# A four-layer graph network on one Trainium2 core: the transposed input comes from 32-feature pieces and VectorE instead of TensorE

## The chip, the cores and the metric

One Trainium2 chip, one of its cores. The metric is the device time of the one launch in microseconds (us). The kernel before takes 2986.86 us (median of three runs, 2981.26 to 2988.62); the profiled execution spans 2982.9 us.

## What is computed

The input `x` has 64 graphs of 256 nodes with 256 features, float32, and `adj` 64 adjacency matrices of 256 by 256, int32. Four layers follow each other, each wrapped as `x = layernorm(x + layer(x))`. Cut to what matters:

```python
# layer 0: masked attention with 8 heads of 32, then a feed-forward part
qkv = x @ Wqkv.T + bqkv
attn = softmax(where(allowed, q k^T / sqrt(32), -inf))
y = layernorm(x + (attn @ v) @ Wo.T + bo)
y = layernorm(y + relu(y @ W1.T + b1) @ W2.T + b2)
# layers 1 and 2: graph attention, e_ij = leaky_relu(f_i + g_j), softmax over neighbours
# layer 3: two relational convolutions with elu
```

The change touches only the first line of layer 0. A matrix product on TensorE sums over the partitions of its two operands, so `x @ Wqkv.T` needs `x` with features on the partitions, while a plain load of `x` puts nodes there. Somewhere `x` has to be turned.

## The kernel before

Each graph is worked out on its own: 256 nodes are two tiles of 128 partitions (`NB = 2`) and 256 features are two blocks of 128 (`KB = 2`). The function `graph(g)` writes down the operations of one graph with, for each, its engine, an assumed cost, the tiles it reads and the tiles it writes. `main_path` does so for all 64 graphs, and `Plan.schedule` then lists the operations of all graphs together in one order. It is a greedy list scheduler that runs while the program is built: each engine takes the ready operation with the earliest due time (graph number times `PERIOD`, less what has to follow), provided that a buffer is free in the ring of each tile it starts. On TensorE it prefers operations of the same mode ("full", "row", "col"). What comes out is a fixed order for each engine's queue; on the chip the engines run these queues in order, with semaphores between them. So operations of several graphs stand interleaved on every engine, and the sizes of the rings (`RINGS`, buffers per tile name) decide how far the graphs may overlap.

The parts of a graph that the change and the prediction touch, with the lines of the profile:

- `load("x", ...)` and `load("adj", ...)` (L582): one 256 KB transfer each, issued from the SyncE queue, rows of 1 KB.
- `masks(adj)` (L643 to L665): `bits` on VectorE (L648), four bfloat16 transposes on TensorE (L653), masks `gm` and `am` on VectorE (L656, L657, L662).
- `transposed(xt)` (L599 to L610): four 128x128 float32 transposes on TensorE into one PSUM bank (L606), and one ScalarE copy of 128x512 to a tile of ring `T` (L609). A graph calls it six times: on `x`, on the attention's output, on the inputs of both graph attentions and of both convolutions. 64 graphs make 384 calls.
- `add_row_later(xt, bo, ...)` (L591): the bias row is added to `x` by an accumulating transfer from the GpSimd queue. `x` is read again only at the end of the attention (L750).
- `projections(xT)` (L667 to L691): twelve products with `Wqkv` on the transposed input, the first TensorE work of a graph that depends on it (L615, names `T,wqkv` and `wqkv,T`).
- `attention` (L693 to L742), `feed_forward` (L753 to L775), where a second copy of `x`, `xr`, gets the row `ln2b` by another accumulating transfer and is added at L597; `gat` (L777 to L814) with tiles `e`, `h` and, in layer 2, `n`; `conv` (L852 to L895).

After the main path a check of ranges (L924 to L937) decides whether a slow general path runs. With these inputs it doesn't; the constants `ones_b` and `eye` are used there alone.

Of the kernel before, what the change touches and what calls it, by code (L numbers as in the profile page):

```python
# [8 lines left out]
F32 = mybir.dt.float32  # L9
F32R = mybir.dt.float32r  # L10
BF16 = mybir.dt.bfloat16
I32 = mybir.dt.int32
# [5 lines left out]
P = 128  # L18
# [3 lines left out]
NO_EDGE = -346.0  # L22


RINGS = {"x": 3, "adj": 4, "bits": 2, "am": 2, "gm": 6, "T": 5, "qk": 2, "v": 2, "p": 12, "both": 4, "inv": 1, "ctxT": 2, "X": 9,
         "xr": 2, "hid": 1, "h": 3, "e": 4, "n": 2, "rel": 3, "hi": 2, "lo": 2, "o": 4}
SMALL = {"mv": 8, "st": 4, "rstd": 8, "r": 6, "rdeg": 4}


# [21 lines left out]
class Plan:  # L51
# [29 lines left out]
    def op(self, engine, cost, issue, graph, reads=(), writes=(), takes=(), mode=None, port=None, lag=None):  # L81


        o = Op(engine, cost, mode, graph, issue, port, lag)
        for accesses, writing in ((reads, False), (writes, True)):
            for a in accesses:
                t, part = a if isinstance(a, tuple) else (a, None)
                write = writing
                if t.ring == "bank":
                    write, part = True, None  # L90
                keys = [k for k in t.parts if part is None or k is None or k == part]
                for k in keys:
                    writer, readers = t.parts[k]
                    o.before.update(readers if write else ())
                    if writer is not None:
                        o.before.add(writer)
                if write:
                    if part is None:
                        t.parts = {}
                    t.parts[part] = (o, [])  # L100
                else:
                    for k in keys or [part]:
                        t.parts.setdefault(k, (None, []))[1].append(o)
                if t not in o.tiles and t.ring is not None:
                    o.tiles.append(t)
        o.tiles += [t for t in takes if t not in o.tiles]
        for t in o.tiles:
            t.left += 1
        o.before.discard(o)
        for b in o.before:  # L110
            b.after.append(o)
        self.ops.append(o)
# [96 lines left out]
def tile_gnn_stack(ctx: ExitStack, tc: tile.TileContext, t: dict, out: bass.AP):  # L209
# [16 lines left out]
    nc = tc.nc  # L226
    x_in, adj_in = t["x"], t["adj"]
    B, N, D = x_in.shape
    assert N == 2 * P and D == 2 * P and B % 2 == 0
    G = B // 2  # L230
    KB = D // P
# [40 lines left out]
    gen = Stage()  # L272
# [6 lines left out]
    def load(st, view, dtype, tag, bufs=1):  # L279
        xt = st.tok(dtype, tag, bufs)  # L280
        nc.sync.dma_start(xt, view)
        return xt
# [15 lines left out]
    def cols(name, n):  # L298

        w = const.tile([P, n], F32, tag=f"col_{name}", name=f"col_{name}")  # L300
        nc.gpsimd.dma_start(w, t[name][0 : n * P].rearrange("(c p) -> p c", p=P))
        return w

    def filled(shape, dtype, tag, value):
        w = const.tile(shape, dtype, tag=tag, name=tag)
        nc.vector.memset(w, value)
        return w
# [13 lines left out]

    ident_b = const.tile([P, P], BF16, tag="ident_b", name="ident_b")
    nc.vector.tensor_copy(ident_b, ident)
    ones_b = filled([P, P], BF16, "ones_b", 1.0)
    ones = filled([P, HD], F32, "ones", 1.0)
    neghalf = filled([P, NT], F32, "neghalf", -0.5)
    eye = filled([P, N // P, N], BF16, "eye", 0.0)
    for h in range(N // P):
        nc.vector.tensor_copy(eye[:, h, h * P : (h + 1) * P], ident_b)
    gcol, bcol = cols("ln1_g", KB), cols("ln1_b", KB)  # L330
    bq = const.tile([P, KB], F32, tag="bq", name="bq")
    nc.vector.tensor_scalar(bq, bqkv[:, 0:KB], scale, None, op0=ALU.mult)
# [11 lines left out]
    for i in (1, 2):  # L344
        a = const.tile([P, 2, KB], F32, tag=f"a{i}", name=f"a{i}")
# [137 lines left out]
    def main_path(plan):  # L483
        x_graph = x_in.rearrange("g (h p) d -> g p h d", p=P)
        adj_graph = adj_in.rearrange("g (h p) m -> g p h m", p=P)
        out_graph = out.rearrange("g (h p) d -> g p h d", p=P)

        def ring(name, bufs):
            plan.ring(name, bufs, lambda shape, dtype, i: pools["work"].tile(shape, dtype, tag=f"{name}{i}", name=name))

        for name, bufs in RINGS.items():
            ring(name, bufs)
# [65 lines left out]
        def graph(g):  # L558
            def op(engine, cost, issue, reads, writes, takes=(), mode=None, port=None, lag=None):
                plan.op(engine, cost, issue, g, reads, writes, takes, mode, port, lag)  # L560

            def pe(mode, cost, issue, reads, writes, takes=()):
                op("PE", cost, issue, reads, writes, takes, mode)
# [4 lines left out]
            def act(cost, issue, reads, writes):  # L568
                op("ACT", cost, issue, reads, writes)
# [4 lines left out]
            def new(ring, shape, dtype=F32):  # L574
                return plan.tile(ring, shape, dtype)

            def tok(ring, dtype=F32):
                return new(ring, [P, NB, D], dtype)

            def load(ring, view, dtype):  # L580
                xt = tok(ring, dtype)
                op("SP", 0.85, lambda: nc.sync.dma_start(xt(), view), [], [xt])  # L582
                return xt
# [9 lines left out]
            def add_row_later(xt, row, reads=()):  # L593
                add_later(xt, lambda: row[:, None, :].to_broadcast([P, NB, D]), reads)
# [4 lines left out]
            def transposed(xt):  # L599

                xT, pt = new("T", [P, KB, N]), new("bank", [P, KB, N])

                def issue():
                    for kb in range(KB):
                        for i in range(NB):
                            nc.tensor.transpose(pt()[:, kb, i * P : (i + 1) * P], xt()[:, i, kb * P : (kb + 1) * P], ident)  # L606

                pe("full", 0.44, issue, [xt], [pt], [xT])
                act(0.47, lambda: nc.scalar.copy(xT(), pt()), [pt], [xT])  # L609
                return xT  # L610

            def product(dst, lhs, rhs, n):
# [203 lines left out]
            def layer1(xt, gm):  # L816
                def finish(i, z, po, r):
                    dve(0.40, lambda: nc.vector.scalar_tensor_tensor(z()[:, i, :], po()[:, 0:D], r(), xt()[:, i, :],
                                                                     op0=ALU.mult, op1=ALU.add), [po, r, xt], [(z, i)])


                z = gat(xt, 0, gm, 2 * g, gbias, finish)
                layer_norm(z)
                return z
# [17 lines left out]
            def relation(adj):  # L842


                rel, other = tok("rel", F32R), tok("e")
                dve(0.33, lambda: nc.vector.tensor_scalar(rel(), adj(), 1.0, None, op0=ALU.is_equal), [adj], [rel], "uses")
                dve(0.60, lambda: nc.vector.scalar_tensor_tensor(
                    other(), adj(), 1.0, rel().bitcast(F32), op0=ALU.not_equal, op1=ALU.mult,
                    accum_out=seen_rel[:, g : g + 1]), [adj, rel], [other], "uses")
                return rel  # L850
# [43 lines left out]
                    [n, o], [o], "uses")  # L894
                return o  # L895

            xt, adj = load("x", x_graph[g], F32), load("adj", adj_graph[g], I32)
            am, gm = masks(adj)
            xT = transposed(xt)
            add_row_later(xt, bo, [c_bo])  # L900
            ctxT = attention(xT, am)
            x1 = product_plus(lambda c: ctxT()[:, c, :], [ctxT, c_wo], lambda c: wo[:, c, :], KB, xt)
            layer_norm(x1)
            xt = feed_forward(x1, load("xr", x_graph[g], F32))
            xt = layer1(xt, gm)
            xt = layer2(xt, gm)
            rel = relation(load("adj", adj_graph[g], I32))
            rdeg = new("rdeg", [P, NB])
            h = conv(conv(xt, 0, rel, rdeg), 1, rel, rdeg)
# [5 lines left out]
        for g in range(B):  # L915
            graph(g)
# [185 lines left out]

    wrong = nc.values_load(bad_i, min_val=0, max_val=4 * P)
    with tc.tile_pool(name="general", bufs=1) as pools["work"], tc.If(wrong > 0):
        w_rel0 = []
        for i in (1, 2):
            w = gen.sb([P, KB, D], F32, f"w_rel0{i}")
            nc.scalar.dma_start(w, t[f"w_rel{i}"][0].rearrange("(c p) n -> p c n", p=P))
            w_rel0.append(w)
        with tc.For_i(0, G) as g:  # L1110
            xt = load(gen, x_view[bass.ds(g, 1)], F32, "x")
            xr = load(gen, x_view[bass.ds(g, 1)], F32, "xr")
            adj = load(gen, adj_view[bass.ds(g, 1)], I32, "adj")
            ctxT = general_attention(transposed(gen, xt), general_mask(adj))
            add_row(xt, bo)
            xt = feed_forward(gen, attention_end(gen, xt, ctxT), xr)
            xt = general_layer1(xt, adj)
            xt = general_layer2(xt, adj)
            xt = general_layer3(xt, adj, w_rel0)
            nc.sync.dma_start(out_view[bass.ds(g, 1)], xt)  # L1120
# [48 lines left out]
```

## Time and profile before

| | before |
|---|---|
| time, median of 3 | 2986.86 us |
| span of the profiled execution | 2982.9 us, 46.6 us for a graph |
| TensorE busy | 2930.1 us, 98% |
| VectorE busy | 2381.6 us, 80% |
| ScalarE busy | 1615.9 us, 54% |
| GpSimd busy | 870.6 us, 29% |
| mean granted TensorE clock | 0.996 |
| moved by DMA | 127.14 MB, 126767 packets |

Every instruction of the profile carries the line of kernel.py that issued it; L615 is the line of nearly all products, so names of operands tell them apart (`bank<-T,wqkv` is a product of the transposed input and the projection weights). A float32 product shows as two records for each instruction of the program, a transpose as one. "Idle before" is the time for which an engine stood still just ahead of a group, with the instruction whose end released it. Records of consecutive matmuls overlap, so the time that a group holds TensorE is read from one group's start to the next group's start in the timeline, not from the sum of durations.

### The profile page before, as it was taken

What the parts mean: (1) busy time and instruction counts of PE and PEld (TensorE: products, weight loads), DVE (VectorE), ACT (ScalarE), POOL (GpSimd) and SP (SyncE); (2) the same over time, 40 slices, a digit from 0 to 9 for tenths busy, and PEclk for the clock granted to TensorE, in tenths of its full rate; (3) what the DMA queues carried; (4) which work ended last, traced back from release to release, by engine and by line L of the source; (5) the groups of instructions that cost most, each with busy time, mean ns of one, the idle gap of its engine ahead of it and who ended that gap; (6) DMA issues with size and microseconds to landing.
All of it is one profiled execution on the core that took longest, in us unless ns stands there. A gap on an engine that the chain in (4) does not pass through costs nothing.

```text
span 2982.9 us, 49733 instructions
## 1 busy us (share of the span) xinstructions
PE 2930.1 (98%) x17462; PEld 2257.1 (76%) x17462; DVE 2381.6 (80%) x6112; ACT 1615.9 (54%) x3905; POOL 870.6 (29%) x2005
## 2 busy tenths in 40 slices
PE   7999999999999999999999999999999999999997
PEld 6777777777777877777777777777777777777884
DVE  5778788788878787878888788787887878879678
ACT  3555555555545555555555555555555554656454
POOL 2232332222232222223322223232232332322232
PEclk9999999999999999999999999999999999999999
DMA  6111121111111211112112111121121211212100
GB/s 166 42 40 44 40 47 39 41 43 36 43 44 28 50 33 47 36 36 51 42 37 47 34 42 43 47 43 30 39 49 41 44 32 40 47 43 44 26 8 23
DMA packets 126767, 127.14 MB, mean 43 GB/s; under 512 B 7697, under 2 KB 125713, under 8 KB 126513
## 3 DMA queue, kind: packets, MB, share of 16 engines
q1 hardware_dynamic: 91072, 89.15, 9.9%
q0 software_dynamic: 35440, 34.76, 8.0%
q8 instruction: 141, 2.31, 0.3%
q14 instruction: 114, 0.93, 0.1%
HBM read 73.54 MB, written 16.78 MB: 30 GB/s over the span
## 4 chain that ended last, share of the span: by engine, by line
PE 82%; DVE 10%; ACT 3%; POOL 3%; issue 1%; DMA 0%; POOLq 0%; DVEq 0%; ACTq 0%
PE bank L615 65%; PE bank L606 5%; PE bank L877 4%; PE bank L709 3%; PE bank L734 3%; PE bank L729 2%; DVE inv L738 1%; ACT X L636 1%; POOL rstd L630 1%; DVE st L624 1%; DVE p L717 1%; PE bank L797 1%; DVE mv L626 1%; DVE o L887 1%; POOL rstd L631 1%
## 5 line engine op out<-in xcount | busy, mean ns | idle before, releaser
L629 POOL TENSOR_SCALAR rstd<-mv 128x2 f32<-128x2 f32 x384 | 108.8, 283 | 1534.1 <-DVE mv L626 1303.8
L636 ACT ACTIVATE X<-X,rstd 128x256 f32<-128x256 f32 x640 | 349.7, 596 | 277.1 <-POOL rstd L632 197.9
L615 PE MATMUL bank<-T,w 128*128 128x256 f32 x2048 | 477.6, 380 | 1.1 <-ACT p L715 1.1
L615 PE MATMUL bank<-cw,T 128*128 128x512 f32 x1024 | 466.6, 598 | 8.8 <-ACT T L609 6.2
L615 PE MATMUL bank<-w,hid 128*128 128x256 f32 x2048 | 461.9, 380 | 1.0 <-ACT p L715 1.0
L615 PEld LDWEIGHTS bank<-w,hid 128*128 128x128 f32 x2048 | 384.1, 190 | 57.6 <-issue 4.6
L615 PEld LDWEIGHTS bank<-T,w 128*128 128x128 f32 x2048 | 377.0, 190 | 52.6 <-ACT T L609 3.3
L717 DVE TENSOR_TENSOR p<-p,am 128x512 f32<-128x512 f32 x512 | 334.2, 681 | 45.1 <-ACT p L715 44.3
L615 PEld LDWEIGHTS bank<-cw,T 128*128 128x128 f32 x1024 | 190.5, 190 | 209.4 <-issue 179.4
L715 ACT ACTIVATE p<-bank 128x512 f32<-128x512 f32 x512 | 300.5, 598 | 48.2 <-PE bank L709 47.8
L630 POOL TENSOR_TENSOR rstd<-rstd,neghalf 128x2 f32<-128x2 f32 x384 | 309.1, 805 | 31.9
L609 ACT COPY T<-bank 128x512 f32<-128x512 f32 x384 | 220.5, 589 | 176.9 <-PE bank L606 174.0
L767 ACT ACTIVATE hid<-bank,col_b 128x256 f32<-128x256 f32 x512 | 210.5, 477 | 118.9 <-PE bank L615 117.9
L615 PE MATMUL bank<-T,wqkv 128*128 128x256 f32 x1024 | 249.0, 386 | 3.5 <-ACT T L609 3.5
L615 PE MATMUL bank<-h,e 128*128 128x259 f32 x1024 | 247.8, 383 | 1.6 <-POOL rstd L632 1.5
L615 PE MATMUL bank<-gw,T 128*128 128x258 f32 x1024 | 247.5, 383 | 1.5 <-ACT T L609 1.3
L624 DVE BATCH_NORM_STATS2 st<-X 128x6 f32<-128x256 f32 x640 | 238.1, 413 | 2.9
L738 DVE RECIPROCAL inv<-bank 128x256 f32<-128x256 f32 x128 | 219.4, 1731 | 13.9 <-PE bank L734 13.9
L615 PEld LDWEIGHTS bank<-h,e 128*128 128x128 f32 x1024 | 190.8, 190 | 52.0 <-issue 23.7
L615 PEld LDWEIGHTS bank<-gw,T 128*128 128x128 f32 x1024 | 190.1, 190 | 39.4 <-issue 7.4
L864 ACT CAST hi<-bank 128x256 fp32r<-128x256 f32 x256 | 95.1, 372 | 228.4 <-PE bank L615 227.0
L615 PEld LDWEIGHTS bank<-T,wqkv 128*128 128x128 f32 x1024 | 190.8, 193 | 34.5 <-ACT T L609 4.8
(124 smaller groups left out, 5028.9 us busy)
## 6 DMA issues: line engine op xcount, KB each, us to landing
adj<-in_adj_dram SPq DMA_DIRECT2D x128, 256.0 KB, 2.8
x<-in_x_dram SPq DMA_DIRECT2D x64, 256.0 KB, 2.7
xr<-in_x_dram SPq DMA_DIRECT2D x64, 256.0 KB, 2.7
xr<-row_ln_b POOLq DMA_DIRECT2D x64, 256.0 KB, 3.9
x<-row_bo POOLq DMA_DIRECT2D x64, 256.0 KB, 4.3
out_dram<-o SPq DMA_DIRECT2D x64, 256.0 KB, 2.1
w<-in_W1T_dram SPq DMA_DIRECT2D x1, 1024.0 KB, 11.1
w<-in_W2T_dram SPq DMA_DIRECT2D x1, 1024.0 KB, 19.4
```

The costliest lines, as they stand in the source:

```text
L606: nc.tensor.transpose(pt()[:, kb, i * P : (i + 1) * P], xt()[:, i, kb * P : (kb + 1) * P], ident)
L609: act(0.47, lambda: nc.scalar.copy(xT(), pt()), [pt], [xT])
L615: nc.tensor.matmul(dst, lhsT=lhs(c), rhs=rhs(c), start=(c == 0), stop=(c == n - 1))
L624: nc.vector.bn_stats(stat()[:, i, :], y()[:, i, :])
L629: nc.gpsimd.tensor_scalar(rstd()[:, 0, :], mv()[:, :, 1], 1.0, EPS, op0=ALU.mult, op1=ALU.add)
L630: nc.gpsimd.tensor_tensor(rstd()[:, 0, :], rstd()[:, 0, :], neghalf[:, 0:NB], op=ALU.pow)
L636: nc.scalar.activation(y()[:, i, :], y()[:, i, :], AF.Identity, bias=rstd()[:, 1, i : i + 1], scale=rstd()[:, 0, i : i + 1])
L715: act(0.58, lambda pr=pr, k=k, sr=s[r]: nc.scalar.activation(pr(), sr(), AF.Exp, accum_out=seen_sum[:, k : k + 1]), [s[r]], [pr])
L717: dve(0.60, lambda pr=pr, kt=kt: nc.vector.tensor_tensor(pr(), pr(), am()[:, kt, None, :].to_broadcast([P, KB, N]), op=ALU.mult), [pr, am] ...
L738: dve(1.62, lambda hg=hg, pc=pc: nc.vector.reciprocal(inv()[:, hg, :], pc()[:, 1, :]), [pc], [(inv, hg)])
L767: act(0.36, lambda f=f, k=k, ph=ph: nc.scalar.activation(hid()[:, f + k, :], ph()[:, k, :], AF.Relu, bias=b1[:, f + k : f + k + 1]), [ph, ...
L877: nc.tensor.matmul(pa()[:, 0:n], lhsT=rel()[:, i, j * P : (j + 1) * P], rhs=part()[:, i, 0:n], start=(c == 0), stop=(c == len(terms) - 1))
```

## The change

The input is turned on the way in. For each of four partition blocks `a` and two feature blocks `kb`, one transfer of 32 KB reads 32 features of all 256 nodes: `blocks[32a + r, kb, m, c]` gets node `32m + r`, feature `128 kb + 32a + c`. Each piece of 32 features is a packet of 128 bytes. One VectorE instruction then transposes every 32x32 block of the 128x512 tile, which puts features on partitions and nodes along the row: the wanted `xT`. TensorE's four transposes and ScalarE's copy for `x` go; the other five calls of `transposed` in a graph stay. `x` itself is still loaded with nodes on partitions for the residual, but later in the graph's list, after the masks.

The new tiles `blocks` (one buffer) and `xT` (two) take room, and rings shrink: `x` 3 to 2, `T` 5 to 4, `X` 9 to 8, `xr` 2 to 1, `e` 4 to 3, `n` 2 to 1. The constants `ones_b` and `eye` move to the general path.

```diff
-RINGS = {"x": 3, ..., "T": 5, ..., "X": 9,
-         "xr": 2, ..., "e": 4, "n": 2, ...}
+RINGS = {"x": 2, ..., "T": 4, ..., "X": 8,
+         "xr": 1, ..., "e": 3, "n": 1, ..., "blocks": 1, "xT": 2}
...
-    ones_b = filled([P, P], BF16, "ones_b", 1.0)
...
-    eye = filled([P, N // P, N], BF16, "eye", 0.0)
...
+            def input_transposed():
+                blocks, xT = new("blocks", [P, KB, N // 32, 32]), new("xT", [P, KB, N])
+                for a in range(4):
+                    for kb in range(KB):
+                        f = kb * P + 32 * a
+                        op("SP", 0.51, lambda a=a, kb=kb, f=f: nc.sync.dma_start(
+                            blocks()[32 * a : 32 * a + 32, kb], x_in[g, :, f : f + 32].rearrange("(m r) c -> r m c", r=32)),
+                           [], [(blocks, 4 * kb + a)])
+                dve(0.62, lambda: nc.vector.transpose(xT().rearrange("p k n -> p (k n)"), blocks().rearrange("p k m c -> p (k m c)")),
+                    [blocks], [xT], "uses")
+                return xT
...
-            xt, adj = load("x", x_graph[g], F32), load("adj", adj_graph[g], I32)
+            xT = input_transposed()
+            adj = load("adj", adj_graph[g], I32)
             am, gm = masks(adj)
-            xT = transposed(xt)
+            xt = load("x", x_graph[g], F32)
             add_row_later(xt, bo, [c_bo])
```

More of the change, by code (lines that the diff above doesn't have):

```diff
@@ L22 @@
 NO_EDGE = -346.0
-RINGS = {"x": 3, "adj": 4, "bits": 2, "am": 2, "gm": 6, "T": 5, "qk": 2, "v": 2, "p": 12, "both": 4, "inv": 1, "ctxT": 2, "X": 9,
-         "xr": 2, "hid": 1, "h": 3, "e": 4, "n": 2, "rel": 3, "hi": 2, "lo": 2, "o": 4}
+RINGS = {"x": 2, "adj": 4, "bits": 2, "am": 2, "gm": 6, "T": 4, "qk": 2, "v": 2, "p": 12, "both": 4, "inv": 1, "ctxT": 2, "X": 8,
+         "xr": 1, "hid": 1, "h": 3, "e": 3, "n": 1, "rel": 3, "hi": 2, "lo": 2, "o": 4, "blocks": 1, "xT": 2}
 SMALL = {"mv": 8, "st": 4, "rstd": 8, "r": 6, "rdeg": 4}
@@ L323, in tile_gnn_stack @@
     nc.vector.tensor_copy(ident_b, ident)
-    ones_b = filled([P, P], BF16, "ones_b", 1.0)
     ones = filled([P, HD], F32, "ones", 1.0)
     neghalf = filled([P, NT], F32, "neghalf", -0.5)
-    eye = filled([P, N // P, N], BF16, "eye", 0.0)
-    for h in range(N // P):
-        nc.vector.tensor_copy(eye[:, h, h * P : (h + 1) * P], ident_b)
     gcol, bcol = cols("ln1_g", KB), cols("ln1_b", KB)
@@ L1104, in tile_gnn_stack @@
     with tc.tile_pool(name="general", bufs=1) as pools["work"], tc.If(wrong > 0):
+        ones_b = gen.sb([P, P], BF16, "ones_b")
+        nc.vector.memset(ones_b, 1.0)
+        eye = gen.sb([P, N // P, N], BF16, "eye")
+        nc.vector.memset(eye, 0.0)
+        for h in range(N // P):
+            nc.vector.tensor_copy(eye[:, h, h * P : (h + 1) * P], ident_b)
         w_rel0 = []
```

## The prediction, made before the changed kernel had run

> **What bounds the kernel now.** I read the busy table first, then the chain of work that ended last, then what TensorE waited for, and at last the timeline around the instructions that go. The page gives the first two:
>
> ```profile
> PE 2930.1 (98%) x17462; PEld 2257.1 (76%) x17462; DVE 2381.6 (80%) x6112; ACT 1615.9 (54%) x3905; POOL 870.6 (29%) x2005
> ...
> PE 82%; DVE 10%; ACT 3%; POOL 3%; issue 1%; DMA 0%; POOLq 0%; DVEq 0%; ACTq 0%
> PE bank L615 65%; PE bank L606 5%; PE bank L877 4%; PE bank L709 3%; PE bank L734 3%; PE bank L729 2%; DVE inv L738 1%; ACT X L636 1%; POOL rstd L630 1%; DVE st L624 1%; DVE p L717 1%; PE bank L797 1%; DVE mv L626 1%; DVE o L887 1%; POOL rstd L631 1%
> ```
>
> TensorE is busy 98% of the span: it is idle 2982.9 - 2930.1 = 52.8 us. The chain runs 82% on TensorE, and no transfer is on it. "Busy" may hide pipelining, so the waits decide. The table of waits of TensorE alone (waiter, releaser: us in total, times, longest):
>
> ```profile
> PE bank L615 <- ACT T L609: 11.0, 14, 1.9
> PE bank L615 <- DVE ctxT L739: 7.6, 1, 7.6
> PE bank L606 <- DMA x<-in_x_dram: 6.2, 1, 6.2
> PE bank L615 <- ACT p L715: 4.9, 9, 1.1
> ```
>
> Two of the four are single waits in the first 50 us (7.6 and 6.2). Between 50 and 2900 us all waits of TensorE together are 19.6 us, 0.7% of that stretch. So in steady state the kernel lasts as long as TensorE's queue is, and a microsecond taken from that queue is worth a microsecond, as long as nothing else becomes late. The groups of TensorE, shapes kept apart, show what the input's transposition is there:
>
> ```profile
> L615 PE MATMUL bank<-T,wqkv 128*128 128x256 f32 x1024 | 249.0, 386 | 3.5 <-ACT T L609 3.5
> L606 PE MATMUL bank<-ident,x 128*128 128x128 f32 x256 | 39.5, 278 | 6.6 <-DMA x<-in_x_dram 6.2 <-PE bank L709 0.4
> ```
>
> 256 transposes, four for each graph, and projections that waited 3.5 us for the copy of a transposed input. The 278 ns are a duration with overlap; what a group of four occupies is read in the timeline (start, length, what):
>
> ```profile
> 482.81 0.60 PE L606 MATMUL bank<-ident,x 128*128 128x128 f32 x4
> 483.24 1.03 PE L615 MATMUL bank<-wo,ctxT 128*128 128x256 f32 x4
> ```
>
> From 482.81 to 483.24 is 0.43 us. Other groups of the same kind read 0.44, a few 0.49 to 0.54 where the work before or after is of another tile mode.
>
> [...] No VectorE transpose is in the trace before. [...]
>
> **Part by part.**
>
> *Removed from TensorE*: 64 groups at 0.44 us = 28.2 us, on the path (98% busy). With the waits of projections for the copy, 3.5 us, it is 31.7 us. The products keep their number: the built program has the same counts of every other TensorE instruction. Its order is new, since the scheduler ran again. In it the tile mode changes 363 times against 376, and the share of the remaining transposes that are followed closely by their own product is about the same (nearly half in both). I read that as an order as dense as before and count nothing for it.
>
> *Removed from ScalarE*: 64 copies of 0.589 us = 37.7 us. ScalarE is busy 54%; worth nothing directly.
>
> *Added to VectorE*: 64 transposes of 128x512. Nearest rows: a one-input operation of that size takes 0.42 us (L891), a two-input one 0.68 us (L717). [...] I take 0.68: 43.5 us, and 2425 us busy, 82%. The bounds are 27 us (0.42) and twice my value, 87 us (84%). All stay below TensorE's 2900, so this lies beside TensorE's work. VectorE's queue is in order: if a transpose waits for its pieces, the masks, softmax products and layer norms of other graphs stand behind it. But `blocks` is refilled as soon as the previous transpose has read it and a graph has 46.6 us, and `xT` has two buffers, so a transpose can run a graph ahead of its projections. Moving `ones_b` and `eye` saves VectorE under 1 us at the start, beside the wait for the first loads.
>
> *Added to the queues*: eight transfers per graph on SyncE at about 0.37 us of issue, as `x` takes there = 3 us of 46.6; that queue mostly waits for buffers. Each has 256 packets, 16 on each DMA engine. Price of a packet: at least q1's 9.9% x 16 x 2982.9 us / 91072 = 52 ns, at most q0's 8.0% x 16 x 2982.9 / 35440 = 108 ns. Eight transfers then hold an engine 128 x 52 to 108 ns = 6.6 to 13.8 us per graph. DMA goes from 18% busy in steady state to 32 to 48%. It is hidden behind the other graphs' TensorE work. In the built order a transfer also waits for the landing of the eighth before it; `x` landed in 3.9 us (median), and eight issues take 3 us, so such a wait is at most a microsecond or two, with nothing urgent behind it.
>
> *Moved*: `x` is loaded later and gets its bias row without waiting for the transposes (the accumulating transfers waited 28.0 us for L606). It is read only after attention: hidden.
>
> *The start*: TensorE began at 6.2 us and its projections at 8.7. Now eight pieces are issued where one load was: about 0.5 us each there, and the eighth waits for `wqkv` to land (4.6 us after 0.74). Last issue near 6, landing near 9, transpose 0.7: projections near 10. The weights' loads stand behind them, some 4 us later. I put +3 us, bounds +1 and +8.
>
> *Rings*: `X` 8, `e` 3, `xr` 1, `n` 1, and a fuller VectorE queue let the graphs overlap less. This is what the profile cannot price. Floor 0; I take a third more of the 19.6 us of steady waits, +6 us.
>
> Sum: 2986.86 - 28.2 - 3.5 + 3 + 6 = 2964.2, so **2964 us**, 0.8% faster.
>
> **Rivals.**
> *The freed time comes back as waits.* Tighter rings make TensorE wait for what a ready tile of another graph used to cover. TensorE's waits for the copy L609 averaged 11.0 / 14 = 0.79 us. A wait like that in two graphs of three is 64 x 0.67 x 0.79 = 34 us: 2986.9 - 31.7 + 3 + 34 = 2992, no change. For it: six rings shrink, and layer 2's single `n` puts its two halves behind each other. Against it: the ordering was made with these rings, and TensorE's order shows no more mode changes. Chance 0.11.
> *Slower: a wait in every graph.* Late pieces stop VectorE's queue, or the single `xr` stops SyncE's and with it the masks' loads. 1.5 waits of 0.79 us per graph are 76 us: 2986.9 - 31.7 + 3 + 76 = 3034; one per graph, 51 us, gives 3009. For it: SyncE is in order and waits often; VectorE at 82% has little slack to catch up. Against it: SyncE's waits before were for buffers, and TensorE waited for a transfer once only, at the start. Chance 0.09.
> *Nothing is added in steady state*: 2986.9 - 31.7 + 1 = 2956. It is the good end of my forecast.
>
> **The numbers.** My forecast 0.80, the first rival 0.11, the second 0.09. 0.3% is 9 us: faster is below 2978, slower above 2996. So faster 0.80, same 0.11, slower 0.09. The range: 2954 (the good end and 2 us) to 2984 (28 us given back instead of 9, between forecast and first rival), which leaves out most of the rivals and a few hundredths below.
>
> **What would show it.** The group L606 with `x` gone, and TensorE's busy time near 2930 - 28 = 2902 with its share still 98%; 64 VectorE transposes near 0.68 us; ScalarE down 38 us; DMA share up by 14 to 30 points with no transfer in TensorE's waits after the first 50 us; waits of TensorE in the middle near 25 us. I am wrong if those waits reach 50 us, with releasers such as `e`, `n`, X or `xT`, or if VectorE's idle time is mostly before the new transpose, ended by the pieces' transfers.

## The result, and the profile after

The changed kernel takes 2941.67 us (median of 4 runs, 2939.83 to 2943.03) against 2984.06 us (4 runs, 2978.51 to 2988.62) for the kernel before on the same chip: a ratio of 0.9858, 95% interval 0.9838 to 0.9878. That is 42 us, 1.4% faster. The forecast was 23 us and the measured time lies below its range. The direction was right and the size was off by nearly a factor of two, so the question of this study is where the other 20 us came from.

The busy table and the chain of the changed kernel, beside those of before:

```profile
span 2939.3 us, 50120 instructions
...
PE 2894.3 (98%) x17206; PEld 2224.7 (76%) x17206; DVE 2415.6 (82%) x6172; ACT 1585.1 (54%) x3841; POOL 861.4 (29%) x2005
...
PE 84%; DVE 8%; POOL 3%; ACT 2%; issue 1%; DMA 1%; SPq 1%; POOLq 0%; DVEq 0%; ACTq 0%
```

TensorE is still the bound at 98%. Its busy time fell by 35.8 us, more than the 28 us of the transposes, and its idle time fell too, from 52.8 to 45.0 us. In the table of TensorE's waits (waiter, releaser: us in total, times, longest) the single wait for the input of the first graph has grown and the wait for `ctxT` at the start has all but gone. Between 90 and 2800 us all waits together fell from 19.3 to 13.6 us:

```profile
PE bank L625 <- DVE xT L618: 11.5, 1, 11.5
PE bank L625 <- ACT T L605: 6.8, 11, 0.9
PE bank L602 <- ACT X L646: 3.6, 8, 1.3
PE bank L602 <- ACT p L725: 3.3, 4, 1.4
...
PE bank L625 <- DVE ctxT L749: 0.6, 1, 0.6
```

(L625 is the line of products, L602 that of transposes, L605 the copy to `T`, as L615, L606 and L609 were before.) The groups on TensorE and VectorE that the change touched, with busy time, mean ns and idle time before them:

```profile
L625 PE MATMUL bank<-xT,wqkv 128*128 128x256 f32 x1024 | 252.8, 386 | 12.8 <-DVE xT L618 11.5 <-ACT T L605 1.4
L618 DVE STREAM_TRANSPOSE xT<-blocks 128x512 f32<-128x512 f32 x64 | 45.0, 703 | 8.7 <-DMA blocks<-in_x_dram 8.1 <-issue 0.4 <-DMA adj<-in_adj_dram 0.2
```

The projections wait for the new transpose once, at the start, and never after. VectorE's transpose takes 703 ns and waits for its pieces in three graphs only (8.1 us in all). The pieces are small on the DMA engines too:

```profile
q1 hardware_dynamic: 230336, 105.96, 13.8%
...
blocks<-in_x_dram SPq DMA_DIRECT2D x512, 32.0 KB, 2.0
```

From 91072 packets at 9.9% of 2982.9 us to 230336 at 13.8% of 2939.3 us: 16 x (405.6 - 295.3) us over 139264 packets is 12.7 ns for each packet more. A piece landed in 2.0 us.

To see when the time was won, I compared the moments at which both traces had finished the same amount of TensorE work (each record counted at the usual distance to its follower, the transposes of `x` at zero). After 90 us the changed kernel is about 6 us ahead; from there to 2890 us the lead grows, unevenly, to 43 us, on average 0.6 us for each graph. A graph's four transposes occupy 0.44 us, 28 us in all. So by this account some 6 us were won at the start, 28 by the transposes, and 9 by something else, of which the shorter waits of the middle are 5.7.

The granted TensorE clock differs too. Over the first 90 us it was 0.92 before and 0.96 in the changed kernel, about 3.6 us of TensorE time by an estimate from these two figures. In the middle the kernel before has one stretch of 3.4 us at about half clock (0.51 from 854.0 to 857.5 us, right behind a wait of 1.9 us), and the changed kernel has none.

### The profile page after: what moved, and what is told of

It reads as the page before. It is cut to its first block, busy times and chain, and to the rows that moved or that the text cites. A ratio compares the mean times of both kernels' runs of the same rounds, so it can differ in the third digit from the quotient of the medians.

```text
span 2939.3 us, 50120 instructions
## 1 busy us (share of the span) xinstructions
PE 2894.3 (98%) x17206; PEld 2224.7 (76%) x17206; DVE 2415.6 (82%) x6172; ACT 1585.1 (54%) x3841; POOL 861.4 (29%) x2005
## 3 DMA queue, kind: packets, MB, share of 16 engines
q1 hardware_dynamic: 230336, 105.96, 13.8%
## 4 chain that ended last, share of the span: by engine, by line
PE 84%; DVE 8%; POOL 3%; ACT 2%; issue 1%; DMA 1%; SPq 1%; POOLq 0%; DVEq 0%; ACTq 0%
PE bank L625 66%; PE bank L602 4%; PE bank L887 4%; PE bank L744 3%; PE bank L719 3%; PE bank L739 2%; POOL rstd L640 1%; DVE st L634 1%; ACT X L646 1%; PE bank L807 1%; DVE o L897 1%; DVE X L760 1%; DVE mv L636 1%; DVE p L727 1%; POOL rstd L639 0%
## 5 line engine op out<-in xcount | busy, mean ns | idle before, releaser
L625 PE MATMUL bank<-T,w 128*128 128x256 f32 x2048 | 480.0, 380 | 1.1 <-ACT T L605 1.1
L625 PE MATMUL bank<-cw,T 128*128 128x512 f32 x1024 | 463.6, 595 | 3.7 <-ACT T L605 2.9
L625 PE MATMUL bank<-w,hid 128*128 128x256 f32 x2048 | 462.5, 380 | 0.0
L625 PEld LDWEIGHTS bank<-w,hid 128*128 128x128 f32 x2048 | 383.6, 190 | 54.7 <-issue 4.0
L625 PEld LDWEIGHTS bank<-T,w 128*128 128x128 f32 x2048 | 378.1, 190 | 59.7 <-issue 8.8
L625 PEld LDWEIGHTS bank<-cw,T 128*128 128x128 f32 x1024 | 191.0, 190 | 200.9 <-issue 181.6
L625 PE MATMUL bank<-xT,wqkv 128*128 128x256 f32 x1024 | 252.8, 386 | 12.8 <-DVE xT L618 11.5
L605 ACT COPY T<-bank 128x512 f32<-128x512 f32 x320 | 185.1, 586 | 144.2 <-PE bank L602 141.4
L625 PE MATMUL bank<-gw,T 128*128 128x258 f32 x1024 | 249.2, 383 | 1.6 <-ACT T L605 1.5
L625 PE MATMUL bank<-h,e 128*128 128x259 f32 x1024 | 249.0, 383 | 0.9 <-ACT e L817 0.3
L625 PEld LDWEIGHTS bank<-xT,wqkv 128*128 128x128 f32 x1024 | 188.2, 191 | 49.0 <-DVE xT L618 11.5
L625 PEld LDWEIGHTS bank<-h,e 128*128 128x128 f32 x1024 | 190.5, 190 | 45.8 <-issue 18.4
L625 PEld LDWEIGHTS bank<-gw,T 128*128 128x128 f32 x1024 | 189.7, 190 | 40.0 <-issue 9.1
```

The source lines that it names most:

```text
L625: nc.tensor.matmul(dst, lhsT=lhs(c), rhs=rhs(c), start=(c == 0), stop=(c == n - 1))
```

## The experiments

All times are medians; "before" stands between 2982 and 2985 us in each set of runs, and each ratio is to it. "Middle" is the sum of TensorE's waits between 90 and 2800 us in the profile; the wait tables shown are of the whole span. The edits are shown as short diffs, in which `...` stands for code that is not shown. Each profile is of one execution. In the expectations, "theory" and "rival" are two answers that the run was to decide between.

### First set: the parts by themselves

**e2_dummy: the TensorE work put back, the order untouched.**

```diff
+ if n == 0:   # first product of the projections
+     for kb in range(KB):
+         for i in range(NB):
+             nc.tensor.transpose(pq()[:, 0, i * P : (i + 1) * P], xT()[:, kb, i * P : (i + 1) * P], ident)
  product(pq()[:, c, :], ...)
```

> The changed kernel in its own order, with four float32 transposes of 128x128 put back on TensorE for each graph: they turn xT into the bank of the first projection, which then overwrites it, so nothing waits for them. Theory: TensorE work is worth its time, 64 x 0.44 = 28 us: 2970 us. Rival (all of the gain of 42 us is TensorE time, because a group with its switches costs 0.66 us): 2984 us. Second rival (the group was partly hidden and the gain comes from elsewhere): under 2958 us.

2964.57 us, 0.9932 (0.9918 to 0.9945): 23 us more than the changed kernel. Its table of waits:

```profile
PE bank L689 <- DVE xT L618: 16.5, 1, 16.5
PE bank L625 <- ACT T L605: 4.5, 8, 0.8
PE bank L602 <- ACT p L731: 3.9, 4, 1.7
PE bank L602 <- ACT X L646: 1.9, 5, 1.0
```

About 4 of the 23 us are a later start (16.5 us, where the first graph's pieces landed later), so 28 us of work cost about 19 behind it. The waits in the middle shrank to 11.2 us from 13.6: the additional work fills a part of them, but that is 2.4 us of the 9. The rest shows as busy time, which rose by only 23.2 us in the whole span (2894.3 to 2917.5), and was not traced further. So TensorE's own time is about half of the 42 us. The remaining 20 us separate two kernels with the same TensorE work.

**e1_rings: the small rings alone.**

```diff
- ... "X": 9, "xr": 2, ..., "e": 4, "n": 2, ...   # kernel before
+ ... "X": 8, "xr": 1, ..., "e": 3, "n": 1, ...
```

> The kernel before, its TensorE transposes of x kept, with only the ring sizes of the change that bind elsewhere: X 8, xr 1, e 3, n 1 (x and T stay as they were). The prediction's step 'Rings' said smaller rings cost about 6 us: 2990. Theory now: the rings cost nothing that can be measured, the new order is as dense as the old, 2984 plus or minus 6 us, with TensorE waits between 50 and 2900 us of 15 to 30 us. Rival: the smaller rings give the scheduler a better order and are where the missing 10 us of gain come from: 2974 or less.

3014.37 us, 1.0098 (1.0082 to 1.0113): 29 us slower. Both theories missed. The waits show what smaller rings do while TensorE turns `x`:

```profile
PE bank L615 <- ACT T L609: 11.7, 16, 1.6
PE bank L615 <- ACT p L715: 10.5, 11, 2.4
PE bank L606 <- ACT X L636: 7.3, 25, 1.1
```

The third was 1.5 us in 5 waits before, and the middle rose from 19.3 to 38.9 us. Other rings also mean another order; the new orders of the kernel before that are drawn further down, with their rings untouched, cost 9 to 12 us, so by that measure most of the 29 goes with the rings. They are no gain in themselves. The changed kernel lives with them, and with fewer waits than before.

**e3_head: one VectorE instruction moved in the kernel before.**

```diff
+ # in the issued order: relation mask of graph 0 behind the last ctxT of graph 0
+ done.insert(at, done.pop(done.index(rel)))
```

VectorE's timeline of the kernel before shows the reason (start, length, instruction, idle time before it and what ended it):

```profile
33.72 0.43 DVE L846 TENSOR_SCALAR rel<-adj 128x512 fp32r<-128x512 int32 x1 [5.03 <-DMA adj<-in_adj_dram]
...
35.46 3.36 DVE L738 RECIPROCAL inv<-bank 128x256 f32<-128x256 f32 x2
38.74 0.69 DVE L739 TENSOR_TENSOR ctxT<-bank,inv 128x256 f32<-128x256 f32 x2
```

The reciprocals of graph 0's attention stood behind `rel`, whose `adj` had not landed. TensorE waited 7.6 us for `ctxT`. In the changed order `rel` comes later, and that VectorE work starts 2.6 us sooner although TensorE began 5 us later:

```profile
32.90 3.36 DVE L748 RECIPROCAL inv<-bank 128x256 f32<-128x256 f32 x2
36.18 0.69 DVE L749 TENSOR_TENSOR ctxT<-bank,inv 128x256 f32<-128x256 f32 x2
```

> The kernel before, with one VectorE instruction moved: the relation mask of graph 0 (tile rel), which waited 5.0 us for the second load of adj at 28.7 us ahead of the reciprocals of graph 0's attention, now stands behind them. Theory: TensorE's wait of 7.6 us for ctxT at 31 us shrinks to about 2.6, and as TensorE bounds the rest the whole kernel ends about 5 us sooner: 2979 us. Rival (a wait at the start is caught up later, since the graphs overlap): 2984 us, the same as before.

2983.66 us, 0.9995 (0.9987 to 1.0004): no difference. The wait did shrink:

```profile
PE bank L606 <- ACT X L636: 5.6, 9, 1.9
PE bank L615 <- ACT p L715: 4.9, 9, 1.1
PE bank L615 <- DVE ctxT L739: 3.3, 1, 3.3
```

7.6 became 3.3, and compared at equal work the lead was 4.2 us from 50 us on to 2000 us. Then 3.7 us of it went between 2100 and 2370 us. In that stretch two waits of transposes for layer norms, which the kernel before does not have there, take 1.9 us (the first line counts the whole span; 2.1 us of it lie in the first 90 us), and the granted clock is 0.99 for 1.00, some 2 us more by estimate. So a gain at the start is carried for most of the run, but a new timing against a fixed order can lose it again in one place. The theory was half right; what the start is worth at the end is not settled by this run.

**e4_dve2: VectorE's transpose twice.**

```diff
+ for _ in range(2):
      nc.vector.transpose(xT()..., blocks()...)
```

> The changed kernel in its own order, with the VectorE transpose of the input run twice in a row (64 x 0.70 = 45 us more on VectorE, busy share 82% to 83.7%). Theory: the transpose is beside TensorE's work, so twice of it costs at most 4 us: 2942 to 2946. Rival (VectorE is near its limit and each microsecond on it delays TensorE's inputs): up to 45 us more, 2960 to 2987.

2954.76 us, 0.9896 (0.9881 to 0.9912): 13 us more. The theory's 4 us were too few and the rival's 18 to 45 too many. In the profile, at equal TensorE work, about 8 us are lost in the middle and the rest at the start, where TensorE began at 15.5 us for 11.5. VectorE at 82% is not free: 45 us of work on it cost TensorE about 8. The waits of the middle rose by only 1.7 us of that (13.6 to 15.3); the rest is in TensorE's busy time (2903.0 us for 2894.3) and was not traced further. The change's own transpose may have cost the like; no run shows it.

### Second set: transfers, rings, and the luck of an order

**e5_dma2: every piece loaded twice.**

```diff
+ for to in (blocks(), extra):
      nc.sync.dma_start(to[32 * a : 32 * a + 32, kb], x_in[g, :, f : f + 32]...)
```

> The changed kernel in its own order, each of the eight pieces loaded twice, the second time to a tile that nobody reads (131072 packets of 128 bytes and 512 issues more). Theory: pieces are hidden in steady state, only the first graph waits longer (eight more issues of 0.55 us ahead of the transpose): 2942 + 4 to 10 us = 2946 to 2952. Rival (small packets hold up the other transfers, adj above all): over 2957, with TensorE or VectorE waits on transfers in the middle of the span.

2958.8 us, 0.9919 (0.9902 to 0.9936), 17 us more; by the figure, the rival. By the trace, neither: from 90 us to 2890 us it loses only 2 us on the changed kernel, and 13 in the first 65 us, in single waits:

```profile
PE bank L629 <- DVE xT L622: 17.5, 1, 17.5
PE bank L629 <- ACT T L606: 6.9, 12, 0.8
PE bank L723 <- DVE gw L524: 4.4, 1, 4.4
```

TensorE began at 17.5 us, the weights, which stand behind the pieces in SyncE's queue, came later too (the wait for `gw` was 4.4 us for 1.5), and the granted clock over the first 90 us was 0.92 for 0.96. In steady state the pieces are hidden even when doubled; at the start they are not.

**e6_wide: the changed kernel with four rings as large as before.**

```diff
- ... "X": 8, "xr": 1, ..., "e": 3, "n": 1, ...   # changed kernel
+ ... "X": 9, "xr": 2, ..., "e": 4, "n": 2, ...
```

> The changed kernel with four of its smaller rings set back to the sizes before (X 9, xr 2, e 4, n 2; x 2 and T 4 stay). With the small rings alone the kernel before became 29 us slower. Theory A (rings of these four names cost time whatever the transposition): 2912 to 2930 us. Theory B (each list order is a lottery of plus or minus 20 us, and rings enter by it alone): anything between 2920 and 2960, no clear sign. Theory C (the changed kernel doesn't need them, as its order has waits of 15 us only): within 4 us of 2942.

2955.29 us, 0.9908 (0.9892 to 0.9925): 14 us slower than with the small rings. Theory A is refuted: to have the four rings large, which was worth 29 us while TensorE turned `x`, is worth nothing without it. Part of the 14 is a start at 14.6 us and a wait of 4.7 us for ScalarE in the first 90 us; the middle is 22.4 us against 13.6, with 3.8 us as the longest single wait. B fits best. This run also limits what follows: without TensorE's transposes of `x`, but with these rings, it gains 27 us on the kernel before (2982.25 us in this set), which is about the removed TensorE work, and its middle is no shorter than the 19.3 us there.

**e7_jit_before, e8_jit_after, and later e12_jit2_before, e13_jit2_after: the same kernels with another order.** One assumed cost of the list scheduler is changed by 4%. No instruction is added, but the order differs from some point on.

```diff
- dve(0.26, diagonal, [am], [am], "uses")
+ dve(0.27, diagonal, [am], [am], "uses")   # 0.25 in e12 and e13
```

> The kernel before with one assumed cost of the list scheduler changed by 4% (the diagonal of the mask, 0.26 to 0.27). No instruction is added or removed, but the order from there on differs. It measures how much a new order by itself is worth. If orders are a lottery: 2984 plus or minus 10 to 30 us. If the order hardly matters: 2984 plus or minus 5.

> The changed kernel with the same 4% change of one assumed cost (0.26 to 0.27). If orders are a lottery and the changed kernel drew a good one: slower, 2945 to 2965. If about 10 us of its gain belong to the change itself (an xT ring of its own, no bank and no ScalarE copy for x) and not to the order: 2942 plus or minus 5 us.

> The kernel before with the assumed cost of the mask's diagonal at 0.25 where it was 0.26 (0.27 gave 11 us more). A second draw of the lottery of orders. If the order of before was a middling draw: 2970 to 3000. If new orders of this kernel stay above it: 2984 to 2995.

> The changed kernel with the assumed cost of the mask's diagonal at 0.25 where it was 0.26 (0.27 gave 2948). A third draw of its orders. Theory (the change gives about 40 us whatever the order): 2938 to 2952. Rival (the changed kernel's order was a lucky one): 2955 to 2970.

| | cost 0.25 | 0.26 (as it is) | 0.27 |
|---|---|---|---|
| kernel before | 2995.93 | 2984.06 | 2993.16 |
| ratio, interval | 1.0036 (1.0024 to 1.0047) | | 1.0036 (1.0024 to 1.0049) |
| middle, us | 28.0 | 19.3 | 28.6 |
| changed kernel | 2944.63 | 2941.67 | 2948.23 |
| ratio, interval | 0.9868 (0.9851 to 0.9886) | 0.9858 (0.9838 to 0.9878) | 0.9880 (0.9864 to 0.9897) |
| middle, us | 13.3 | 13.6 | 14.5 |

A new order alone moves the time by 3 to 12 us. But the two kernels don't overlap: the orders of one have 19 to 29 us of waits in the middle, those of the other 13 to 15. The kernel before was not unlucky; its order is the best of its three. So the 20 us belong to the change, with its rings, and not to one lucky draw: between the means of the three orders of each lie 46 us, not 42. Three orders of each are few, and e6 shows one without TensorE's transposes of `x` at 2955 us.

### Third and fourth set: what of the old chain costs the other 20 us

The change removed a chain: `x` loaded early and held until the residual sum, four transposes on TensorE, a bank (`bank` in the tables, which TensorE writes), a ScalarE copy, a buffer of `T`. These runs put parts of it back or give the kernel before more room for it.

**e10_act: only the ScalarE copy put back, the order untouched.**

```diff
+ if n == 0:
+     nc.scalar.copy(extra, xT())
  nc.scalar.activation(qk()[:, n, :], ...)
```

> The changed kernel in its own TensorE order, with a ScalarE copy of xT (128x512) to a tile that nobody reads, just ahead of the first eviction of the projections: 64 x 0.59 = 38 us put back on ScalarE, nothing on TensorE. Theory A (the ScalarE copy that went had delayed other evictions, and this is part of the missing 10 us): 2942 + 5 to 12 us. Theory B (ScalarE is 54% busy and the copy was beside other work): within 4 us of 2942.

2948.45 us, 0.9876 (0.9859 to 0.9892). By the median this is theory A. The trace is of the fastest of the four executions (2943.86 us; the others took 2948.3 to 2948.8): there the middle is 12.9 us against 13.6 and the same work takes 0.7 us more from 90 to 2890 us, while TensorE began at 15.7 us for 11.5. That speaks for B, the copy being beside other work, but what the three slower executions lost is not in it. The copy costs between nothing and 7 us; that is left open.

**e11_first: graph 0 turned on TensorE.**

```diff
+ if g == 0:
+     xt, adj = load("x", ...), load("adj", ...)
+     am, gm = masks(adj)
+     xT = transposed(xt)
+ else:
      xT = input_transposed()
      ...
```

> The changed kernel, but graph 0 is turned on TensorE as before, the other 63 by pieces and VectorE; the list order is new from the start on. In the changed kernel TensorE began at 11.5 us, in the kernel before at 6.2. Theory (the first pieces delay the start, and that delay lasts to the end): TensorE begins at 6.2 us, and 3 to 6 us are won, 2936 to 2939, give or take the 7 us that a new order alone has shown. Rival (the start is waited for elsewhere, by the weights and adj): 2942 or more.

2941.89 us, 0.9854 (0.9838 to 0.9871): the same as the changed kernel; the rival. TensorE began at 6.2 us and then waited:

```profile
PE bank L602 <- DMA x<-in_x_dram: 6.2, 1, 6.2
PE bank L625 <- DVE ctxT L749: 6.0, 1, 6.0
```

What is won at the first wait is lost at the next one: at the start the chain through the first graph's attention sets the pace, whichever engine turns `x`. The granted clock over the first 90 us is 0.92 again, as in the kernel before.

**e9_pe_turn and e14_pe_turn_x3: the change's rings, but TensorE turns x.** The way of turning is set back, and with it the early load of `x`; `xT` keeps its own ring. The second has a third `x` buffer.

```diff
- xT = input_transposed()        # pieces, VectorE
+ xT = input_transposed(xt)      # plain load, four transposes into a bank, ScalarE copy to xT
...
- RINGS = {"x": 2, ...           # e9
+ RINGS = {"x": 3, ...           # e14
```

> The changed kernel's rings (x 2, T 4, X 8, xr 1, e 3, n 1 and an xT ring of two for the transposed input), but x is turned as before: one plain load, four TensorE transposes into a bank, one ScalarE copy into xT. Only the way of turning separates it from the changed kernel. Theory A (28 us of TensorE time, and about 10 us because x then needs no bank, no ScalarE copy and no chain across three engines): 2942 + 38 = 2980. Theory B (nothing but TensorE time, the rest is the lottery of orders): 2942 + 23 to 28 = 2965 to 2970, with the lottery of 5 to 15 us on top. Theory C (small rings are bad whenever TensorE turns x, as in the kernel before with small rings): 3010.

3114.27 us, 1.0427 (1.041 to 1.0445). None of the theories had that.

```profile
PE bank L602 <- DVE o L901: 22.7, 15, 1.8
PE bank L602 <- ACT X L644: 19.9, 27, 3.2
PE bank L623 <- ACT T L605: 17.7, 28, 1.1
PE bank L623 <- ACT xT L617: 11.3, 17, 2.0
```

TensorE waits everywhere (83.3 us in the middle). Its waits are not the whole price: the granted clock of this profile is 0.986 where the kernel before has 0.996, about 31 us of 3119 by an estimate from these figures. In the trace of the kernel before, the time from a load of `x` to its residual sum (kth load to kth sum, graphs 5 to 59) is 137.9 us at a period of 45.8: three buffers, always in use. In the changed kernel it is 90.3 us at 45.3, two buffers always in use, but there nothing waits for an early `x`; its projections take the pieces. Full buffers alone do not show a shortage: with four `x` buffers (e15 below) the time is 184.9 us at 46.0, all four in use, and nothing is gained.

> As the run with TensorE turning x on the changed kernel's rings, which took 3114 us, but with three x buffers where that had two. Theory (x is held from its early load for the transposition to the residual sum after attention, which kept three buffers full in the kernel before, so two were the bound): 2985 to 3020, near the kernel before with small rings (3014). Rival (the other small rings make the 3114): over 3080.

3016.17 us, 1.0104 (1.0085 to 1.0123), as the theory said. The third buffer was worth 98 us while TensorE turns `x`, and what is left is the price of the other small rings that e1 had shown (middle 38.5 and 38.9 us).

**e15_x4 and e18_T6: the kernel before with more room.** Both move the two constants to make it.

```diff
- RINGS = {"x": 3, ..., "T": 5, ...
+ RINGS = {"x": 4, ..., "T": 5, ...   # e15
+ RINGS = {"x": 3, ..., "T": 6, ...   # e18
```

> The kernel before with four x buffers where it has three, and ones_b and eye moved to the general path as in the change to make room. In its trace a new load of x starts the moment the residual sum frees a buffer, so three are always in use. Theory (the x ring of three still held back the overlap of graphs, and the change gained by taking x out of it): 2965 to 2975. Rival (three were enough, as the transposes stand 40 us behind their load): within the spread of new orders, 2980 to 2996.

> The kernel before with six T buffers where it has five (constants moved to make room, as in the change). In the change x no longer passes through T: five uses per graph and four buffers, against six and five. Theory (T was short, and relief of it is part of the 20 us): 2960 to 2975. Rival (T is not short, or a new order costs as much): 2980 to 3000, as the three other new orders of the kernel before.

3000.25 us, 1.0050 (1.0032 to 1.0069), and 2992.80 us, 1.0024 (1.0013 to 1.0036). The theories fell: neither a fourth `x` nor a sixth `T` brings the kernel before below its own time. Both runs also have a new order, which alone cost 9 to 12 us above, so a gain of a few us could hide in them; a shortage worth 10 or 20 us does not show.

**e16_planned: the dummy work of e2, told to the scheduler.**

```diff
- pe("full", 0.86, issue, [xT, c_wqkv], [pq], [qk])
+ pe("full", 0.86 + 0.44 * (n == 0), issue, [xT, c_wqkv], [pq], [qk])
```

> The changed kernel with four dummy transposes on TensorE per graph, as in the earlier run (2965 us), but with their 0.44 us told to the list scheduler, so that the order is made for this load. Theory (the TensorE time itself is worth 23 to 28 us, and the other 20 us to the kernel before are the chain load, TensorE, bank, ScalarE that x no longer goes through): 2960 to 2975. Rival (the order made with the additional TensorE work is what was worse before): 2980 to 2996.

2958.71 us, 0.9916 (0.9898 to 0.9933). A new order that counts on the work is no worse than the old one; the work costs less in it (middle 9.4 us). TensorE's time for the transposes is worth 17 to 23 us by these two runs. Waits of this kernel:

```profile
PE bank L689 <- DVE xT L618: 12.9, 1, 12.9
PE bank L625 <- ACT T L605: 7.4, 8, 1.4
PE bank L689 <- ACT p L731: 2.0, 7, 0.3
```

**e17_chain: a chain like the old one, planned.** The pieces and VectorE's transpose stay. `xT` is turned once more on TensorE into a bank of its own and copied by ScalarE to a tile that no instruction reads; only the scheduler believes that the projections need it.

```diff
+ junk, pt = new("junk", [P, KB, N]), new("bank", [P, KB, N])
+ pe("full", 0.44, turn_back, [xT], [pt], [junk])
+ act(0.47, lambda: nc.scalar.copy(junk(), pt()), [pt], [junk])
...
- ... [xT, c_wqkv], [pq], [qk])
+ ... [xT, junk, c_wqkv], [pq], [qk])
```

> The changed kernel with a chain like the one it removed, planned: xT is turned again by four TensorE transposes into a bank of its own and copied by ScalarE to a tile junk; the list scheduler is told that the projections need junk, though on the chip they don't wait for it. Turning by pieces and VectorE stays. Theory (the 20 us that are not TensorE time belong to the chain's bank, ScalarE slot and place in the order): 2975 to 2995, as the kernel before. Rival (they don't; dummies without bank and copy gave 2959 and 2965): 2955 to 2970, and then the difference lies in what x's own tile has to do besides, its early load, its place in the x and T rings.

3020.09 us, 1.0124 (1.0107 to 1.0141): worse than even the theory said, 61 us above e16, which has the same work on TensorE and VectorE and none of bank, copy and planned dependence. Its table of waits, without those of the start:

```profile
PE bank L602 <- ACT X L646: 25.6, 28, 3.4
...
PE bank L625 <- ACT T L605: 6.4, 10, 0.9
PE bank L625 <- ACT e L817: 5.5, 5, 1.8
PE bank L887 <- DVE lo L875: 4.3, 4, 1.5
```

TensorE waits 25.6 us for layer norms' outputs on ScalarE, in 28 places, against 0.3 us in e16. The middle is 45.6 us against 9.4, and the granted clock 0.993 against 0.997, about 12 us by estimate. The projections themselves do not wait for the junk copy, so what is left is the order that the chain makes the scheduler choose and the bank and the ScalarE time that it takes on the chip. Which of the parts (the bank, the slot on ScalarE, the place of the projections in the order) does it was not separated. The rings are the small ones, and the kernels with such a chain and these small rings take about the same (3014 us in e1, 3016 in e14, 3020 here), but for e9 with its two `x` buffers. How much of the 61 us a chain costs with the rings of the kernel before, this run does not tell.

## Why the prediction was off

Point by point, by its own steps:

- **The bound.** Right. TensorE's queue sets the time, busy 98% in both kernels, and the runs that added 28 us to the changed kernel's became slower (by 17 us in e16, 23 in e2).
- **Removed from TensorE, 28.2 us and 3.5 us of waits.** The mechanism was right, the size was high: putting the work back costs 17 us (e16) to 23 us (e2), so a microsecond of it was worth about 0.6 to 0.8. Only 2.4 to 4.2 us of the difference are waits of the middle that it filled; the rest is open.
- **"I read that as an order as dense as before and count nothing for it."** This is the step that failed, together with the next one: the two put the waits of the middle at about 25 us, and they were 13.6. Mode changes and the neighbourhood of transposes and products looked alike, and they did not show density. Kernels with TensorE in the input's chain waited 19 to 30 us in the middle in five orders (38 and more with small rings), kernels without it 9 to 16 us in all nine runs with the change's rings, which are five orders; with wider rings (e6) it was 22.4. From e16 and e2 to the kernel before, with the same TensorE work, it is 19 to 25 us. That the waits go with the chain and the rings is shown; why its removal makes for a denser order is not.
- **Rings, +6 us.** Wrong sign as part of the sum, where the waits of the middle fell by 5.7 us, and wrong in its reason. Small rings cost 29 us while TensorE turns `x` (e1), and widening them without that chain made the kernel 14 us slower (e6). The step had to be taken together with the chain that fills those rings, not added to it.
- **The start, +3 us.** Its parts were right: TensorE began 5.2 us later (11.5 for 6.2; the seven other runs with the same first nine transfers in this order 12.9 to 16.5, so this was the earliest of eight). Its sum was not, because the 7.6 us wait for `ctxT`, which stood in the second table that the prediction showed, all but went with the new order; with it the granted clock of the first 90 us rose from 0.92 to 0.96, about 3.6 us by estimate. At 90 us the changed kernel was about 6 us ahead, where the step had it 3 behind. e3 and e11 show that the start as a whole isn't a sum of its waits.
- **The sum.** The start, the rings and the order make up about the whole miss of 22.5 us: the start was off by 9 us, the waits of the middle by 12, and 3 more come in because the kernel before measured 2984.06 us in the result for the 2986.86 of the forecast. It is a count from the two profiles; e2 and e16 divide the gain otherwise, with less for TensorE's time and more for the order.
- **Added to VectorE, hidden.** Duration right, 0.703 us for 0.68. That it would go like the slower of the two rows was my estimate; nothing in the trace of before showed it. Hiding not quite: a second one of the same length cost about 8 us in the middle (e4).
- **Pieces hidden.** Right in steady state (e5: 2 us for twice the pieces), and the price of a packet was far too high: 12.7 ns more for each, where I had 52 as a floor. The share of the DMA engines in the middle went from 0.18 to 0.22, not to 0.32 or more. A packet of 128 bytes is not as dear as one of 1 KB. By bytes it is still slower: by an estimate from the q1 lines of both pages, 10 GB/s per engine (128 B in 12.7 ns) where the packets of before, most of 1 KB, made 20 (1024 B in 52 ns).
- **ScalarE, -37.7 us, worth nothing directly.** It fell by 31 us. By e10 the copy as such is worth between nothing and 7 us.
- **The rivals.** Both let the freed time come back as waits. The waits of the middle fell instead. No case of mine had a gain beyond the removed work, so the range ended 12 us too high.

## What to carry to other kernels

When an order is made by a scheduler, count what a removed step asked of it, not only its time on the busiest engine: here the removal of a step across three engines, with a bank and a held buffer, gave about as much besides its TensorE time as by it. A ring's size is only right or wrong for the chains that pass through it, so don't add up a change's small rings and its removed chain as if they were independent. Before a difference of 0.3% is explained, draw the order again: a 4% change of one assumed cost moved these kernels by 3 to 12 us. And when waits are added up, look at the granted clock too: in e9 its estimated share was half as large as the added waits.

## What the runs showed of the hardware that was not expected

- 139264 packets more, of which 131072 are the pieces' of 128 bytes, cost 12.7 ns each on the DMA engines, while those of before, most of 1 KB, came to 52 ns.
- In six profiles the granted clock was the lower, the longer TensorE waited: with 9.4, 13.6, 19.3, 38.9, 45.6 and 83.3 us in the middle (e16, the changed kernel, the kernel before, e1, e17, e9) it was 0.997, 0.997, 0.996, 0.994, 0.993 and 0.986. The order is not strict: e14 had 0.992 with 38.5 us. A thousandth of these spans is about 3 us. In the kernel before, a single wait of 1.9 us was followed by 3.4 us at about half clock (0.51 from 854.0 to 857.5 us).
- A float32 transpose of 128x512 in 32x32 blocks took 703 ns on VectorE, 692 to 712 in 64 cases.
- The start varied: with the same first nine transfers TensorE's first instruction came at 11.5 to 16.5 us in eight profiles, one of each kernel.
